# A transformer block on one core: int8 rows set apart, token copies on POOL, maxima over partitions by a PE transposition

## The chip, the cores and the metric

The kernel runs on one core of a Trainium2 chip. A core has TensorE (PE, matmuls; the load of a stationary operand is listed as PEld), VectorE (DVE), ScalarE (ACT), GpSimd (POOL) and SyncE (SP, which here issues DMAs). Each works through its own queue in order, and semaphores hold an instruction back until what it needs is done. [...] The metric is the device time of one execution in microseconds; a comparison takes the median of several runs.

## The reference

The input `x` is 64 sequences of 64 tokens with 256 features, float32. One block is computed:

```python
x = x + attention(rotate(x, delta, amplitudes, frequencies), W_qkv, W_o, log_gamma)
x = x + ffn(masked_pooling(x, W1, b1, v, itok), clip_x, clip_down, w_gate, w_up, w_down)

def act_fake_quant(x, clip):                 # ONE scale for the whole tensor
    scale = sigmoid(clip) * max(abs(x)) / 127
    return clip_(round(x / scale), -128, 127) * scale

def ffn(x, ...):
    xq   = act_fake_quant(x, clip_x)
    gate = xq @ weight_fake_quant(w_gate).T  # 256 -> 704
    up   = xq @ weight_fake_quant(w_up).T
    h    = act_fake_quant(silu(gate) * up, clip_down)
    return h @ weight_fake_quant(w_down).T   # 704 -> 256
```

What matters here is that each activation quantization needs the largest absolute value of a whole tensor, 4096 tokens by 256 and 4096 by 704, before one element of it can be quantized. The two maxima cut the feed-forward part into stages.

## The kernel before

The 4096 tokens are eight groups of 512 (`NG = 8`, `GW = 512`); a group is four tiles of 128 tokens. The first part of the kernel, up to about 239 us of the profile, is attention and the masked pooling, a software pipeline over the groups. It writes the pooled tokens, transposed (features on partitions), to `pooled[g]`, 128 partitions by 2 by 512, float32, and for every group's halves a column of partial maxima to `xam`. The change touches the part after that.

*First scale.* `act_scale(xam, 0, ...)` (lines 96 to 105) reduces `xam` along its row to `mx`, one value per partition, on DVE; POOL's `partition_all_reduce` (line 101) gives every partition the largest of the 128; two small DVE operations make the scale `sx` and its reciprocal `rx`. Ahead of that, ACT loads the table for Silu by a dummy activation (`warm`, line 944).

*Gate stage.* `quantize_tokens(g)` lets ACT multiply a group by `rx` and round it to int8 (`x8`, line 954), and DVE widen that to bf16 (`xq`, line 955). Then come four passes (`j`) over pairs of groups, each over six chunks (`c`) of 128 of the 704 inner features; the last chunk has 64, and the pair's two groups share its 128 partitions. For a chunk PE makes `pg` (gate) and `pu` (up) in PSUM, two buffers each, eight matmuls of 512 columns together (line 978). ACT writes `gate = silu(pg)` (line 986). The product `h` goes to `hT[j]`, by one of two paths: for the chunks in a list, ACT copies `pu` to `up` (line 993) and POOL multiplies (line 996); for the others DVE multiplies straight out of PSUM (line 998). The list has ten of the 24. DVE then takes the largest absolute value of each product into a column of `ham` (`largest`, line 958), two chunks late. After chunks 1 and 3 a group of the next pass is quantized.

*Second scale.* `act_scale(ham, 1, ...)`, the same way, gives `sh` and `rh`.

*Down stage.* `quantize(g)` rounds a group's 704 inner features to int8 on ACT (`h8`, named `h` in the profile, line 1033) and widens it to bf16 on DVE (`hq`, line 1034): five full chunks in one instruction, 5 rows of 512, and for an even group one instruction more, ahead of it, for the shared last chunk of the pair. The first and the last group are done in two halves of 256 tokens. The int8 buffer of a group is 6 rows of 512 bytes without a gap, while in `hq` and `hT` the rows of the pair's two groups alternate, so that a group's rows lie 1024 elements apart there. `down(g)` then multiplies with `wdT`, 24 matmuls of 256 columns (line 1047), scales the result on DVE in two instructions (line 1054) and sends it off. Seven groups go out by a DMA from POOL that adds to what stands in the output (line 1063); the residual was written there earlier. The last group is added on DVE (line 1059) and written by SP in two halves (line 1060).

The order is written out: `manual_schedule` fixes the named engines' queues to the program's order, ACT and DVE in the feed-forward part. PE and POOL there are ordered by a scheduler. In the down stage the program runs `quantize(g)` ahead of `down(g - 1)`.

Of the kernel before, what the change touches and what calls it, by code (L numbers as in the profile page):

```python
# [9 lines left out]
F32 = mybir.dt.float32  # L10
BF16 = mybir.dt.bfloat16
I32 = mybir.dt.int32
I8 = mybir.dt.int8
# [4 lines left out]
P = 128  # L18
# [8 lines left out]
def adaln_attn_ffn(  # L27
# [65 lines left out]
    wscale = const.tile([P, 2, NC], F32, name="wscale")  # L93
    dsc = const.tile([P, D], F32, name="dsc")

    def act_scale(cols, k, scale, inv):

        mx = const.tile([P, 1], F32, name=f"mx{k}")
        nc.vector.tensor_reduce(mx, cols, AX.X, ALU.max)
        allmx = const.tile([P, 1], F32, name=f"allmx{k}")  # L100
        nc.gpsimd.partition_all_reduce(allmx, mx, P, bass_isa.ReduceOp.max)  # L101
        nc.vector.tensor_scalar(
            scale, allmx, csig[:, k : k + 1], 1.0 / QMAX, ALU.mult, ALU.mult
        )
        nc.vector.reciprocal(inv, scale)  # L105


    with ExitStack() as actx:
# [25 lines left out]
        def bank(name):  # L134
            return ps.tile([P, 512], F32, tag="bank", name=name)
# [776 lines left out]
        pooling(a, (1,))  # L912
        pooling_out(a, (1,))


    with ExitStack() as fctx:
        fp = fctx.enter_context(tc.tile_pool(name="ffn", bufs=1))


        assert 2 * LAST == P  # L920
        NP = NG // 2
        NF = 2 * (NC - 1)
        ps_f = ctx.enter_context(ExitStack())
        fw = ps_f.enter_context(tc.tile_pool(name="ffnw", bufs=2))
        ps_g = ps_f.enter_context(
            tc.tile_pool(name="ps_g", bufs=2, space=bass.MemoryType.PSUM)
        )
        xq = fp.tile([P, 2, NT], BF16, name="xq")
        hT = [
            (fp if j < NP - 1 else big).tile(  # L930
                [P, NF + 1, GW], F32, tag=f"hT{j}" if j < NP - 1 else "last", name=f"hT{j}"
            )
            for j in range(NP)
        ]
        ham = fp.tile([P, NP * NC], F32, name="ham")
        ordered = ctx.enter_context(ExitStack())
        ordered.enter_context(
            tc.manual_schedule(
                engines={mybir.EngineType.Activation, mybir.EngineType.DVE}
            )  # L940
        )

        warm = fp.tile([P, 1], F32, name="warm")
        nc.scalar.activation(warm, xam[:, 2 * NG + 1 : 2 * NG + 2], AF.Silu)
        sx = fp.tile([P, 1], F32, name="sx")
        rx = fp.tile([P, 1], F32, name="rx")
        act_scale(xam, 0, sx, rx)
        wsx = fp.tile([P, 2, NC], F32, name="wsx")
        nc.vector.tensor_scalar_mul(wsx, wscale, sx)

        def quantize_tokens(g):

            x8 = fw.tile([P, 2, GW], I8, tag="x8", name=f"x8_{g}")
            nc.scalar.activation(x8, pooled[g], AF.Copy, scale=rx)  # L954
            nc.vector.tensor_copy(xq[:, :, g * GW : (g + 1) * GW], x8)  # L955

        def largest(j, c, h):
            nc.vector.tensor_reduce(  # L958
                ham[:, j * NC + c : j * NC + c + 1], h, AX.XY, ALU.max,
                apply_absolute_value=True,  # L960
            )

        quantize_tokens(0)
        quantize_tokens(1)


        late = []
        for j in range(NP):
            for c in range(NC):
                wide = c < NC - 1  # L970
                n = 2 if wide else 1
                pg = ps_g.tile([P, 2, GW], F32, tag="pg", name=f"pg_{j}_{c}")
                pu = ps_g.tile([P, 2, GW], F32, tag="pu", name=f"pu_{j}_{c}")
                for dst, w in ((pg, wgT), (pu, wuT)):
                    for kc in range(2):
                        for k in range(2):
                            g = 2 * j + k
                            nc.tensor.matmul(  # L978
                                dst[:, k, :] if wide else dst[k * LAST : (k + 1) * LAST, 0, :],
                                w[:, kc, c * P : min((c + 1) * P, FF)],  # L980
                                xq[:, kc, g * GW : (g + 1) * GW],
                                start=(kc == 0),
                                stop=(kc == 1),
                            )
                gate = fw.tile([P, 2, GW], F32, tag="gate", name=f"gate_{j}_{c}", bufs=3)
                nc.scalar.activation(  # L986
                    gate[:, :n], pg[:, :n], AF.Silu, scale=wsx[:, 0, c : c + 1]
                )
                h = hT[j][:, 2 * c : 2 * c + n, :]

                if wide and c in ((0, 2, 4), (1, 3), (0, 2, 4), (0, 2))[j]:
                    up = fw.tile([P, 2, GW], F32, tag="up", name=f"up_{j}_{c}")
                    nc.scalar.activation(  # L993
                        up, pu, AF.Copy, scale=wsx[:, 1, c : c + 1]
                    )
                    nc.gpsimd.tensor_tensor(h, gate, up, ALU.mult)  # L996
                else:
                    nc.vector.scalar_tensor_tensor(  # L998
                        h, pu[:, :n], wsx[:, 1, c : c + 1], gate[:, :n], ALU.mult, ALU.mult
                    )  # L1000
                late.append((j, c, h))
                if len(late) > 2:
                    largest(*late.pop(0))
                if c in (1, 3) and j + 1 < NP:
                    quantize_tokens(2 * (j + 1) + c // 2)
        for l in late:
            largest(*l)
        ps_f.close()
        fw = fctx.enter_context(tc.tile_pool(name="ffnd", bufs=2))
        ps_d = fctx.enter_context(  # L1010
            tc.tile_pool(name="ps_d", bufs=4, space=bass.MemoryType.PSUM)
        )

        sh = fp.tile([P, 1], F32, name="sh")
        rh = fp.tile([P, 1], F32, name="rh")
        act_scale(ham, 1, sh, rh)

        hq = {}

        def quantize(g):  # L1020

            j, k = divmod(g, 2)
            if k == 0:
                hq[j] = fw.tile([P, NF + 1, GW], BF16, tag="hq", name=f"hq_{j}")
            h8 = fw.tile([P, NC, GW], I8, tag="h8", name=f"h8_{g}")
            parts = 2 if g in (0, NG - 1) else 1
            for r in range(parts):
                cols = slice(r * (GW // parts), (r + 1) * (GW // parts))
                for rows, tmp in (
                    (slice(NF, NF + 1), h8[:, NC - 1 : NC, cols]),  # L1030
                    (slice(k, NF, 2), h8[:, 0 : NC - 1, cols]),
                )[k:]:
                    nc.scalar.activation(tmp, hT[j][:, rows, cols], AF.Copy, scale=rh)  # L1033
                    nc.vector.tensor_copy(hq[j][:, rows, cols], tmp)  # L1034

        def down(g):
            j, k = divmod(g, 2)

            res = xg[0 if g == NG - 1 else g]
            for r in range(2):  # L1040
                tiles = slice(2 * r, 2 * r + 2)
                pdn = ps_d.tile([P, 2, D], F32, tag="pdn", name=f"pdn_{g}_{r}")
                for i in range(2):
                    tok = slice((2 * r + i) * P, (2 * r + i + 1) * P)
                    for c in range(NC):
                        half = slice(0, P) if c < NC - 1 else slice(k * LAST, (k + 1) * LAST)
                        nc.tensor.matmul(  # L1047
                            pdn[:, i, :],
                            hq[j][half, 2 * c + k if c < NC - 1 else NF, tok],
                            wdT[half, c, :],  # L1050
                            start=(c == 0),
                            stop=(c == NC - 1),
                        )
                nc.vector.tensor_tensor(  # L1054
                    res[:, tiles], pdn, dsc.unsqueeze(1).to_broadcast([P, 2, D]), ALU.mult
                )
                if g == NG - 1:
                    xr = xg[g][:, tiles, :]
                    nc.vector.tensor_tensor(xr, xr, res[:, tiles], ALU.add)  # L1059
                    nc.sync.dma_start(out=ot[g][:, tiles, :], in_=xr)  # L1060
            if g < NG - 1:

                nc.gpsimd.dma_start(out=ot[g], in_=res, accum_op=ALU.add)

        for g in range(NG + 1):
            if g < NG:
                quantize(g)
            if g == 0:
                nc.vector.tensor_scalar_mul(dsc, dsc, sh)
            else:  # L1070
                down(g - 1)
        ordered.close()
# [44 lines left out]
```

## Time and profile before

| what | value |
|---|---|
| median of three runs | 339.9 us (339.25 to 340.07) |
| the profiled execution, own time | 340.35 us |
| its span, first to last instruction | 338.6 us |
| granted PE clock, mean | 0.959 |
| busy: PE, DVE, ACT, POOL | 285.5, 253.8, 197.6, 77.8 us |
| first scale, `mx` starts | 239.3 us |
| gate stage, first `x8` to last maximum | 240.7 to 295.0 us |
| second scale, `rh` ends | 296.1 us |
| down stage, first `h` to the last DVE instruction | 296.2 to 333.9 us |

All times come from one profiled execution. A group row of the profile names line, engine, operation, output and inputs, shapes and count; behind the bar stand the busy time, the mean of one in ns, and the idle time of the engine ahead of it with what ended it. A timeline row gives start and duration in us and merges like instructions; in brackets stands the idle time ahead of it. Lines of the changed kernel have other numbers; the names stay.

### The profile page before, as it was taken

What the parts mean: (1) busy time and instruction counts of PE and PEld (TensorE: products, weight loads), DVE (VectorE), ACT (ScalarE), POOL (GpSimd) and SP (SyncE); (2) the same over time, 40 slices, a digit from 0 to 9 for tenths busy, and PEclk for the clock granted to TensorE, in tenths of its full rate; (3) what the DMA queues carried; (4) which work ended last, traced back from release to release, by engine and by line L of the source; (5) the groups of instructions that cost most, each with busy time, mean ns of one, the idle gap of its engine ahead of it and who ended that gap; (6) DMA issues with size and microseconds to landing.
All of it is one profiled execution on the core that took longest, in us unless ns stands there. A gap on an engine that the chain in (4) does not pass through costs nothing. (4 is left out here: it accounts for less than half of the span.)

```text
span 338.6 us, 8695 instructions
## 1 busy us (share of the span) xinstructions
PE 285.5 (84%) x3762; PEld 194.5 (57%) x3762; DVE 253.8 (75%) x510; ACT 197.6 (58%) x299; POOL 77.8 (23%) x72
## 2 busy tenths in 40 slices
PE   0499999999999999989999999784499889168892
PEld 0386768668668758848858858563243334034451
DVE  6569886886976974884883783856359999969993
ACT  1566458568477483673673573332598798196620
POOL 0051330240240230112012021040055358003331
PEclk9999999999999999999999999997599999859997
DMA  5491721001001001000100100100000000005999
GB/s 157 118 339 34 202 73 62 5 2 64 3 2 63 4 0 42 26 2 3 66 0 2 66 2 11 56 0 3 2 0 0 1 2 0 0 0 67 131 123 177
DMA packets 16789, 16.15 MB, mean 48 GB/s; under 512 B 2160, under 2 KB 16496, under 8 KB 16752
## 3 DMA queue, kind: packets, MB, share of 16 engines
q1 hardware_dynamic: 12480, 11.83, 11.3%
q0 software_dynamic: 3696, 3.67, 8.1%
q8 instruction: 29, 0.48, 0.6%
q10 hardware_dynamic: 576, 0.11, 0.2%
q14 instruction: 8, 0.07, 0.1%
HBM read 7.74 MB, written 7.86 MB: 46 GB/s over the span
## 5 line engine op out<-in xcount | busy, mean ns | idle before, releaser
L334 DVE TENSOR_TENSOR at<-psc,gam 128x512 f32<-128x512 f32 x64 | 39.7, 681 | 14.6 <-PE psc L321 14.6
L1047 PE MATMUL pdn<-wdT,hq 128*128 128x256 bf16 x192 | 30.4, 291 | 13.2 <-DVE hq L1034 13.2
L386 PE MATMUL po<-woT,yT 128*128 128x256 f32 x128 | 31.1, 386 | 5.2 <-DVE kn L252 2.7
L152 POOL TENSOR_TENSOR ys<-x,cs 128x1024 f32<-128x1024 f32 x7 | 13.8, 1967 | 89.8 <-DVE xr L166 67.4
L1047 PEld LDWEIGHTS <-hq 128*128 128x128 bf16 x192 | 16.7, 101 | 27.2 <-DVE hq L1034 14.8
L206 PE MATMUL pk<-wkT,xT 128*128 128x256 f32 x128 | 30.0, 388 | 0.2 <-ACT xT L196 0.2
L978 PE MATMUL pg<-xq,wgT 128*128 128x512 bf16 (+1 forms) x96 | 25.1, 391 | 5.9 <-DVE xq L955 5.1
L206 PE MATMUL pv<-wvT,xT 128*128 128x256 f32 x128 | 29.8, 386 | 0.1
L996 POOL TENSOR_TENSOR hT<-gate,up 128x1024 f32<-128x1024 f32 x10 | 24.1, 2410 | 24.0 <-ACT up L993 24.0
L386 PEld LDWEIGHTS po<-woT,yT 128*128 128x128 f32 x128 | 23.1, 190 | 11.2 <-DVE kn L252 5.1
L281 PE MATMUL pq<-xT,wqT 128*128 128x512 f32 x64 | 29.5, 604 | 0.0
L1033 ACT ACTIVATE h<-hT,rh 128x2560 int8<-128x2560 f32 (+3 forms) x15 | 22.2, 1538 | 12.5 <-DVE rh L105 7.0
L986 ACT ACTIVATE gate<-pg,wsx 128x1024 f32<-128x1024 f32 (+1 forms) x24 | 25.0, 1053 | 6.0 <-PE pg L978 3.6
L978 PE MATMUL pu<-xq,wuT 128*128 128x512 bf16 (+1 forms) x96 | 24.6, 390 | 2.3 <-ACT up L993 1.3
L206 PEld LDWEIGHTS pk<-wkT,xT 128*128 128x128 f32 x128 | 24.2, 195 | 3.9 <-ACT xT L196 0.9
L958 DVE TENSOR_REDUCE ham<-hT 128x1 f32<-128x1024 f32 (+1 forms) x24 | 26.3, 1118 | 0.0
L206 PEld LDWEIGHTS pv<-wvT,xT 128*128 128x128 f32 x128 | 23.7, 190 | 4.5 <-issue 1.4
L408 POOL TENSOR_TENSOR bias<-pre,sel 128x256 f32<-128x256 f32 x8 | 4.9, 612 | 86.7 <-DVE ms L457 86.7
L1034 DVE CAST hq<-h 128x2560 bf16<-128x2560 int8 (+3 forms) x15 | 22.2, 1509 | 3.2 <-ACT h L1033 3.2
L289 ACT ACTIVATE qbd<-pq,hm 128x512 f32<-128x512 f32 x32 | 20.1, 680 | 4.9 <-PE pq L281 4.8
L321 PE MATMUL psc<-qbd,kT 32*64 32x128 f32 x1024 | 20.7, 279 | 0.6 <-DVE at L334 0.3
L998 DVE SCALAR_TENSOR_TENSOR hT<-pu,wsx,gate 128x1024 f32<-128x1024 f32 (+1 forms) x14 | 15.7, 1124 | 6.3 <-ACT gate L986 6.3
(177 smaller groups left out, 530.4 us busy)
## 6 DMA issues: line engine op xcount, KB each, us to landing
x<-in_x_dram SPq DMA_DIRECT2D x8, 512.0 KB, 6.4
out_dram<-x SPq DMA_DIRECT2D x7, 512.0 KB, 3.9
out_dram<-x POOLq DMA_DIRECT2D x7, 512.0 KB, 6.1
wq_nat<-in_L_attn_W_qkv_dram SPq DMA_DIRECT2D x3, 256.0 KB, 8.8
wnat_d<-in_L_ffn_w_down_dram SPq DMA_DIRECT2D x1, 704.0 KB, 7.0
wnat<-in_L_ffn_w_gate_dram SPq DMA_DIRECT2D x1, 640.0 KB, 4.9
wnat<-in_L_ffn_w_up_dram SPq DMA_DIRECT2D x1, 640.0 KB, 6.6
out_dram<-x SPq DMA_DIRECT2D x2, 256.0 KB, 4.3
```

Of the source, the lines that this page charges most:

```text
L206: nc.tensor.matmul(pk[:, i * D : (i + 1) * D], xT[:, kc, t * P : (t + 1) * P], w[:, kc, :], start=(kc == 0), stop=(kc == 1),)
L281: nc.tensor.matmul(pq, wqT[:, kc, hf * P : (hf + 1) * P], xT[:, kc, :], start=(kc == 0), stop=(kc == 1),)
L321: nc.tensor.matmul(banks[p][k * S : (k + 1) * S, i, hf, :], kT[rows, hf, b * S : (b + 1) * S], qbd[rows, hf, b].rearrange("p k t -> p (k t)"),
L334: nc.vector.tensor_tensor(at[:, p].rearrange("p i f k t -> p i (f k t)"), banks[p].rearrange("p i f c -> p i (f c)"), gam[:, p] .rearrange ...
L386: nc.tensor.matmul(po[:, i * D : (i + 1) * D], yT[:, i, hf].rearrange("p k t -> p (k t)"), woT[:, hf, :], start=(hf == 0), stop=(hf == 1),)
L958: nc.vector.tensor_reduce(ham[:, j * NC + c : j * NC + c + 1], h, AX.XY, ALU.max, apply_absolute_value=True,)
L978: nc.tensor.matmul(dst[:, k, :] if wide else dst[k * LAST : (k + 1) * LAST, 0, :], w[:, kc, c * P : min((c + 1) * P, FF)], xq[:, kc, g * G ...
L986: nc.scalar.activation(gate[:, :n], pg[:, :n], AF.Silu, scale=wsx[:, 0, c : c + 1])
L996: nc.gpsimd.tensor_tensor(h, gate, up, ALU.mult)
L1033: nc.scalar.activation(tmp, hT[j][:, rows, cols], AF.Copy, scale=rh)
L1034: nc.vector.tensor_copy(hq[j][:, rows, cols], tmp)
L1047: nc.tensor.matmul(pdn[:, i, :], hq[j][half, 2 * c + k if c < NC - 1 else NF, tok], wdT[half, c, :], start=(c == 0), stop=(c == NC - 1),)
```

## The change

Five edits go together.

- `act_scale` gets a PSUM tile. PE transposes `mx`, read as 128 equal columns, against the identity, so that every partition holds all 128 values in a row, and DVE reduces that row. `partition_all_reduce` goes. The first call, with `warm`, moves to the end of the attention part's written-out order; `pmx_0` takes one of that part's PSUM banks, `pmx_1` a buffer of the down stage's pool.
- The first two groups' tokens are quantized in four pieces, feature half by feature half, with four `x8` buffers; they are widened on DVE. `wsx` comes after them in DVE's queue.
- The other six groups' widening copies are POOL's, whose queue is now written out too: a copy comes after the multiplies that stand ahead of it in the program.
- The list of chunks multiplied on POOL is chunks 0, 2, 4 in even passes and 1, 3 in odd ones: again ten, in the last pass 1 and 3 in place of 0 and 2.
- `h8` has rows of 576, of which 512 are used. The first group is rounded and widened in pieces of 128, 128 and 256 tokens.

```diff
-    def act_scale(cols, k, scale, inv):
+    def act_scale(cols, k, scale, inv, pt):
         mx = const.tile([P, 1], F32, name=f"mx{k}")
         nc.vector.tensor_reduce(mx, cols, AX.X, ALU.max)
         allmx = const.tile([P, 1], F32, name=f"allmx{k}")
-        nc.gpsimd.partition_all_reduce(allmx, mx, P, bass_isa.ReduceOp.max)
+        nc.tensor.transpose(pt, mx.to_broadcast([P, P]), ident)
+        nc.vector.tensor_reduce(allmx, pt, AX.X, ALU.max)
...
+        warm = const.tile([P, 1], F32, name="warm")
+        nc.scalar.activation(warm, xam[:, 2 * NG + 1 : 2 * NG + 2], AF.Silu)
...
+        act_scale(xam, 0, sx, rx, bank("pmx_0")[:, 0:P])
...
-                engines={mybir.EngineType.Activation, mybir.EngineType.DVE}
+                engines={
+                    mybir.EngineType.Activation,
+                    mybir.EngineType.DVE,
+                    mybir.EngineType.Pool,
+                }
...
-        nc.vector.tensor_scalar_mul(wsx, wscale, sx)
-        def quantize_tokens(g):
-            x8 = fw.tile([P, 2, GW], I8, tag="x8", name=f"x8_{g}")
-            nc.scalar.activation(x8, pooled[g], AF.Copy, scale=rx)
-            nc.vector.tensor_copy(xq[:, :, g * GW : (g + 1) * GW], x8)
+        def quantize_tokens(g, kcs=slice(0, 2)):
+            x8 = fw.tile([P, 2, GW], I8, tag="x8", name=f"x8_{g}_{kcs.start}", bufs=4)
+            nc.scalar.activation(x8[:, kcs], pooled[g][:, kcs], AF.Copy, scale=rx)
+            widen = nc.vector if g < 2 else nc.gpsimd
+            widen.tensor_copy(xq[:, kcs, g * GW : (g + 1) * GW], x8[:, kcs])
+        for kc in range(2):
+            for g in range(2):
+                quantize_tokens(g, slice(kc, kc + 1))
+        nc.vector.tensor_scalar_mul(wsx, wscale, sx)
...
-                if wide and c in ((0, 2, 4), (1, 3), (0, 2, 4), (0, 2))[j]:
+                if wide and c in ((0, 2, 4), (1, 3))[j % 2]:
...
-        act_scale(ham, 1, sh, rh)
+        pmx = ps_d.tile([P, P], F32, tag="pmx", name="pmx_1", bufs=1)
+        act_scale(ham[:, 0:nham], 1, sh, rh, pmx)
...
-            h8 = fw.tile([P, NC, GW], I8, tag="h8", name=f"h8_{g}")
-            parts = 2 if g in (0, NG - 1) else 1
-            for r in range(parts):
-                cols = slice(r * (GW // parts), (r + 1) * (GW // parts))
+            h8 = fw.tile([P, NC, GW + 64], I8, tag="h8", name=f"h8_{g}")
+            at = 0
+            for n in (1, 1, 2) if g == 0 else (2, 2) if g == NG - 1 else (4,):
+                cols = slice(at * P, (at + n) * P)
+                at += n
```

`largest` now counts its own columns, which changes no instruction.

More of the change, by code (lines that the diff above doesn't have):

```diff
@@ L913, in adaln_attn_ffn @@
         pooling_out(a, (1,))
+        warm = const.tile([P, 1], F32, name="warm")
+        nc.scalar.activation(warm, xam[:, 2 * NG + 1 : 2 * NG + 2], AF.Silu)
+        sx = const.tile([P, 1], F32, name="sx")
+        rx = const.tile([P, 1], F32, name="rx")
+        act_scale(xam, 0, sx, rx, bank("pmx_0")[:, 0:P])
     with ExitStack() as fctx:
@@ L938, in adaln_attn_ffn, with largest @@
             tc.manual_schedule(
-                engines={mybir.EngineType.Activation, mybir.EngineType.DVE}
-            )
-        )
[L943 to L947, printed above, removed]
-        wsx = fp.tile([P, 2, NC], F32, name="wsx")
-        nc.vector.tensor_scalar_mul(wsx, wscale, sx)
-        def quantize_tokens(g):
-            x8 = fw.tile([P, 2, GW], I8, tag="x8", name=f"x8_{g}")
-            nc.scalar.activation(x8, pooled[g], AF.Copy, scale=rx)
-            nc.vector.tensor_copy(xq[:, :, g * GW : (g + 1) * GW], x8)
-        def largest(j, c, h):
+                engines={
[3 more added lines that the diff above has]
+                }
+            )
+        )
+        wsx = fp.tile([P, 2, NC], F32, name="wsx")
+        def quantize_tokens(g, kcs=slice(0, 2)):
[6 more added lines that the diff above has]
+                quantize_tokens(g, slice(kc, kc + 1))
+        nc.vector.tensor_scalar_mul(wsx, wscale, sx)
+        nham = 0
+        def largest(h):
+            nonlocal nham
             nc.vector.tensor_reduce(
-                ham[:, j * NC + c : j * NC + c + 1], h, AX.XY, ALU.max,
-                apply_absolute_value=True,
-            )
-        quantize_tokens(0)
-        quantize_tokens(1)
+                ham[:, nham : nham + 1], h, AX.XY, ALU.max, apply_absolute_value=True
+            )
+            nham += 1
         late = []
@@ L1000, in adaln_attn_ffn @@
                     )
-                late.append((j, c, h))
+                late.append(h)
                 if len(late) > 2:
-                    largest(*late.pop(0))
+                    largest(late.pop(0))
                 if c in (1, 3) and j + 1 < NP:
                     quantize_tokens(2 * (j + 1) + c // 2)
-        for l in late:
-            largest(*l)
+        for h in late:
+            largest(h)
         ps_f.close()
```

## The prediction

> **What bounds the kernel now.** I read the page first, for its chain, then the groups kept apart by shape, then the timeline of the last 100 us, and last the table of windows, for the DMA.
>
> ```profile
> span 338.6 us, 8695 instructions
> DVE hq L1034 4%; ACT gate L986 3%; PE pdn L1047 2%; DVE x L1054 2%; PE pg L978 2%; ACT x L954 2%; PE pu L978 2%; ACT h L1033 2%; ACT up L993 2%; DVE hT L998 1%; POOL hT L996 1%; DVE xq L955 0%; DVE ham L958 0%; DVE x L1059 0%; POOL allmx L101 0%
> ```
>
> The costliest line of the chain is the widening copy `hq<-h`. Its shapes, from the groups of the last 100 us (name, shapes, count, then busy us and mean ns):
>
> ```profile
> L1034 DVE CAST hq<-h 128x2560 bf16<-128x2560 int8 x6 | 16.9, 2812 | 1.1 <-ACT h L1033 1.1
> L955 DVE CAST xq<-x 128x1024 bf16<-128x1024 int8 x8 | 7.0, 870 | 1.7 <-ACT x L954 1.7
> L1034 DVE CAST hq<-h 128x1280 bf16<-128x1280 int8 x4 | 3.9, 985 | 1.5 <-ACT h L1033 1.5
> L684 POOL TENSOR_SCALAR_AFFINE_SELECT gam<-gam 64x1024 f32<-64x1024 f32 x2 | 2.3, 1148 | 1.8 <-ACT gam L681 1.7
> ```
>
> Twice the elements (1280 to 2560) cost 2.9 times the time: 1.10 ns each against 0.77. The down stage, one pair of groups, from the timeline (start, duration, engine):
>
> ```profile
> 304.71 1.28 DVE L1054 TENSOR_TENSOR x<-pdn,dsc 128x512 f32<-128x512 f32 x2
> 305.91 3.14 DVE L1034 CAST hq<-h 128x512 bf16<-128x512 int8 x2
> 308.97 1.28 DVE L1054 TENSOR_TENSOR x<-pdn,dsc 128x512 f32<-128x512 f32 x2
> 309.11 3.53 PE L1047 MATMUL pdn<-wdT,hq 128*128 128x256 bf16 x24 [0.73 <-DVE hq L1034]
> 310.16 2.81 DVE L1034 CAST hq<-h 128x2560 bf16<-128x2560 int8 x1
> 312.89 1.28 DVE L1054 TENSOR_TENSOR x<-pdn,dsc 128x512 f32<-128x512 f32 x2
> 313.03 3.52 PE L1047 MATMUL pdn<-wdT,hq 128*128 128x256 bf16 x24 [0.40 <-DVE hq L1034]
> ```
>
> DVE runs without a hole: 304.71 to 312.89 is 8.18 us for two groups, 4.09 each. PE needs 3.49 a group (`325.46 6.98`, x48, in the same view) and waits for `hq` at each. So DVE bounds this stage.
>
> The gate stage, 240.74 to 294.97, has the same owner: from 248.60 on, DVE's idle entries add up to 1.3 us in 46. PE's last matmul ends at 288.8; then DVE works off multiplies and maxima until 294.97. One line shows what the tokens' copies cost there:
>
> ```profile
> 260.55 2.42 POOL L996 TENSOR_TENSOR hT<-gate,up 128x1024 f32<-128x1024 f32 x1 [2.39 <-ACT up L993]
> 261.54 1.98 DVE L955 CAST xq<-x 128x1024 bf16<-128x1024 int8 x1
> 264.76 1.02 PE L978 MATMUL pu<-xq,wuT 128*128 128x512 bf16 x4 [0.82 <-DVE hT L998]
> ```
>
> A copy of 0.68 us took 1.98: it ended 0.5 us after POOL's multiply did. PE then stood 0.82 us.
>
> [...]the whole int8 block is one run of 2560 while its destination has 5 rows[...]; the half-width pieces are 5 rows of 256 on both sides[...] The multiply here takes 2.41 us for 1024; POOL's one-input select takes 1.15.
>
> **The change, part by part.** Times after `rh` or `rx` are taken from those instructions' ends (296.11 and 240.43).
>
> *Rows set apart.* `h8` rows become 576 wide, so source and destination are both 5 rows of 512[...]. In the steady pairs DVE then needs 8.18 - 2 x 1.06 = 6.06 us, PE 6.98, ACT (2.42 + 0.72 + 2.42, each overlapping the next by 0.1) 5.3. PE becomes the bound, with about 0.7 us to spare before each copy is missed. ACT's rows are strided now; I charge nothing, its half-width forms (1.35 us for 1280) lie on the same line as 2560 (2.42).
>
> *First group in pieces 1, 1, 2.* ACT's rows give 0.29 + 0.83 ns an element. Small piece 0.40, then 5 x 128 in 0.82[...]: PE starts 0.10 + 0.30 + 0.82 + 0.05 + 0.55 + 0.05 = 1.87 us after `rh`, before 2.91. At PE's half clock a 128-token tile takes 1.43 (5.73 / 4). The third tile waits for the 1280 copy (4.9), so the group ends at 7.8. Group 1 needs ACT's sixth and seventh pieces (end 6.2, with two instructions more, 0.3 us later than now) and 1.75 of copy: PE starts it at 8.05, before 8.74. **-0.7.** Seven groups follow: before 304.85 to 332.46 = 27.6, after 7 x 3.49 = 24.4. **-3.2.**
>
> *What the writes give back.* Each group's accumulating DMA is already close behind the last one:
>
> ```profile
> core 0: us, PE busy (x) PEld busy (x) DVE busy (x) ACT busy (x) POOL busy (x), PEclk, DMA share, GB/s
> 320.00:324.00 4.00, 3.60 (x26) 2.08 (x25) 4.00 (x5) 2.92 (x3) 1.27 (x1) 1.00 0.98 130
> 334.00:335.00 1.00, 0.00 (x0) 0.00 (x0) 0.00 (x0) 0.00 (x0) 0.00 (x0) 1.00 1.24 200
> ```
>
> Seven DMAs take 8.1% of the span, 3.9 us of all engines each; with a group every 3.49 us they queue. If 3.9 is firm, 7 x 3.9 plus the last two writes ends only 0.7 us earlier than now, and 3.2 us are lost. But the last row carries 200 GB/s where the steady ones carry 130, so some of 3.9 is latency that a queue hides. Bounds 0 to 3.2; I take **+0.6**. POOL's issue (1.28 us) took 1.52 and 1.59[...]; 0.3 us on a DMA that queues anyway: nothing.
>
> *Maxima by PE.* Now `mx` end to `sx` start is 0.56 us (239.46 to 240.02), and 0.55 the second time. In its place: a transposition and a PSUM reduction of 128 columns. The transposition of `pp` near 236 took 0.63 from DVE's end to DVE's next start, a 128-column reduction 0.28: 0.94. First time, +0.38 less the 0.31 us that ACT's table load already runs past `rx` (ACT starts at 240.74): **+0.1**. Second time PE is at half clock after 5 us of rest: +0.4 to 0.6, **+0.45**. Bounds 0 and 1.0 in all. On PE nothing but the next stage's matmuls is queued behind either transposition; they need its result anyway. On POOL the all-reduce stood ahead of the hidden multiplies and of the output DMAs, hundreds of nanoseconds that nobody waited for.
>
> *Tokens in four half copies.* Two ACT pieces of 0.72 in place of 1.15, DVE 0.42 in place of 0.69: PE starts 1.25 us after ACT does, before 1.9; the fourth piece arrives at 3.1 as before at 2.9. The first gate starts some 0.7 earlier. `wsx` waits behind four copies and still comes before the first gate.
>
> *Six copies to POOL.* DVE loses 0.87 + 0.68 + 1.98 + 3 x 0.68 = 5.6 us (5.1 without overlaps). POOL gains six copies; no row shows one[...]. I take 1.15, the select's row. POOL's order is multiply, copy, multiply: `x8_5` stands behind the multiply of pass 1's fourth chunk, so PE waits there about 1.2 us. I laid all rows of this stage in queue order with 0.05 us per hand-over. For before this ends 54.4 us after ACT's start (measured 54.23), for after 52.4: PE's holes at `pu<-hT` shrink, ACT becomes near-critical (pass 0 holds 10.8 us of ACT work, PE's 48 matmuls 10.35), and the tail from the last gate (two multiplies' remainder and three maxima, 4 us) stays. **-1.9**, start included. At 1.6 us a copy this is -0.7; at 2.0, +1.4; at 2.4, +3.8. Ten multiplies stay on POOL, the last pass has chunks 1 and 3 in place of 0 and 2.
>
> Sum: -0.7 - 3.2 + 0.6 + 0.1 + 0.45 - 1.9 = **-4.65**. The profiled execution took 340.35 (1.75 around its span): 335.7. It lay 0.45 above the median of the three runs, 339.9, from which the forecast is **335.3**. Less than 0.3%, 1.0 us, can't be told from no change here.
>
> **Rivals.** *POOL's copy is dear* (the one that ends slower): above 2.2 us each, PE waits for `xq` at all three pass borders and ACT behind it, and -1.9 turns into over +2.7. At 2.4: -4.65 + 5.7, 341.0. For it: POOL's two-input rows, and int8 may be dearer than f32; against: the select. *The copy stays[...]* (the rows apart don't count): no 3.2, group 1 starts 0.4 later instead of 0.7 earlier; with the rest -1.0, 338.9. Against it stand the 985 ns rows, whose source already lies apart. *The writes bind*: 2.6 more given back, 337.9. For it the DMA share of 0.98, against it the 200 GB/s.
>
> **How the numbers follow.** Forecast 0.66 (own range 334.2 to 336.8: the writes and PE's clock, which leaves half speed at a varying moment, ±0.7 us); writes bind 0.15; dear copy 0.12 (a third of it still faster, at 1.5 to 1.8 us)[...]. Range 333.3 to 338.7. Faster: 0.66 + 0.15 + 0.03 + 0.01 = 0.85; same 0.06[...]; slower 0.09.
>
> **What would show it.** Casts of 2560 at 1.75 us, and PE without a hole from group 1 to 7 (else the first step is wrong). The first `pdn` matmul 1.9 us after `rh`. POOL's copies near 1.15; if over 2, holes before `pg` at each pass. `sh` 0.9 to 1.1 us after `mx`. The gate stage from ACT's start to the last `ham` near 52.4. DMA share at 1 up to the end with the last landing later than 5.5 us after PE's end would mean the writes bind.

## The result, and the profile after

The changed kernel takes **337.05 us** (median of four, 336.96 to 337.29). The kernel before takes 339.66 beside it (339.25 to 340.07). The ratio is 0.9924, 95% interval 0.9907 to 0.9942: faster by 2.6 us. The forecast was 335.3, 4.6 us under the median then known (339.9). The measured time lies inside the range of 333.3 to 338.7 but above the forecast's own 334.2 to 336.8. The profiled execution took 336.96, its span is 3.4 us shorter. The page's first line and its chain by lines:

```profile
span 335.2 us, 8697 instructions
...
PE po L388 9%; PE pv L208 9%; PE pdn L1060 7%; PE pk L208 6%; PE psc L323 4%; PE py L361 4%; DVE at L336 4%; ACT gate L997 3%; ACT L238 3%; PE pl L511 3%; DMA afb<-n_L_cond_amplitudes_dram 3%; PE pa L433 2%; POOL hT L1006 2%; ACT up L1003 2%; DVE xam L528 2%
```

The widening copy `hq`, 4% of the span in the chain before, no longer stands among these lines: one cast of 1.77 us is left of it, ahead of PE's start on group 1. PE's `pdn` has 7%, 2% before. (The list before followed the chain back only to 240.8 us, this one to the start of the kernel, so the other lines can't be set against each other.) The groups of the last 100 us, by shape (count, then busy us and mean ns):

```profile
L1047 DVE CAST hq<-h 128x2560 bf16<-128x2560 int8 x6 | 10.5, 1750 | 1.1 <-ACT h L1046 1.1
...
L961 POOL CAST xq<-x 128x1024 bf16<-128x1024 int8 x6 | 6.2, 1036 | 0.0
```

2812 ns has become 1750, as the forecast had it. By the access patterns that the trace keeps for these casts, the int8 source was one run of 2560 and is now 5 rows of 512, like the destination in both kernels; that this alone makes the difference, experiments 2 and 3 show. POOL's copy takes 1036. The down stage in the timeline, the last piece of group 0 and the first groups after it:

```profile
304.78 8.39 PE L1060 MATMUL pdn<-wdT,hq 128*128 128x256 bf16 x58 [0.25 <-DVE hq L1047]
...
305.83 2.08 DVE L1047 CAST hq<-h 128x512 bf16<-128x512 int8 x2
...
309.02 1.75 DVE L1047 CAST hq<-h 128x2560 bf16<-128x2560 int8 x1
...
311.80 0.69 DVE L1067 TENSOR_TENSOR x<-pdn,dsc 128x512 f32<-128x512 f32 x1 [0.44 <-PE pdn L1060]
```

From 304.78 PE runs on without a wait, and it is DVE that waits for PE (the last line). The two have changed places. The table of windows, with the DMA's share behind the clock:

```profile
core 0: us, PE busy (x) PEld busy (x) DVE busy (x) ACT busy (x) POOL busy (x), PEclk, DMA share, GB/s
...
324.00:328.00 4.00, 4.00 (x30) 2.30 (x28) 2.65 (x4) 0.00 (x0) 1.95 (x2) 1.00 1.21 181
```

The gate stage shows what went wrong. Its first six microseconds:

```profile
240.42 2.56 ACT L959 ACTIVATE x<-pooled_a,rx 128x512 int8<-128x512 f32 x4 [0.62 <-DVE rx L107]
...
242.55 1.06 PE L989 MATMUL pg<-xq,wgT 128*128 128x512 bf16 x2 [0.22 <-issue]
...
243.40 0.63 PE L989 MATMUL pu<-xq,wuT 128*128 128x512 bf16 x1
...
243.83 1.06 PE L989 MATMUL pg<-xq,wgT 128*128 128x512 bf16 x2
...
246.25 1.11 ACT L997 ACTIVATE gate<-pg,wsx 128x1024 f32<-128x1024 f32 x1 [3.28 <-PE pg L989]
```

PE is never idle here for long, and yet ACT's first gate starts 5.83 us after the first `x8`. PE's queue deals out `pg_0`, `pu_0` and `pg_1` in turn. (By the order of the weight loads, an entry of `x2` holds one matmul of `pg_1` and one of `pg_0`; the record of the first `pu` is missing.) So the fourth matmul of `pg_0`, which releases the gate, is PE's tenth. PE is at half clock here (the granted clock is 0.5 until 246.05), and a matmul takes 0.43 us. In the kernel before the gate waited for PE's fifth matmul.

Where the time went, from the two profiled executions:

| stretch | before | after | difference | forecast |
|---|---|---|---|---|
| up to `mx` of the first scale (same code) | 239.29 | 238.82 | -0.47 | 0 |
| first scale, `mx` to ACT's first `x8` | 1.45 | 1.60 | +0.15 | +0.1 |
| gate stage, to the last `ham` | 54.20 | 54.71 | **+0.5** | **-1.9** |
| second scale, `mx` end to `sh` | 0.55 | 0.96 | +0.41 | +0.45 |
| `rh` end to PE's start of group 1 | 8.74 | 8.07 | -0.67 | -0.7 |
| seven groups on PE | 27.61 | 24.27 | -3.34 | -3.2 |
| PE's end to the end of the span | 6.14 | 6.15 | 0.0 | +0.6 |

The rows add up to -3.4. The medians differ by 2.6, since the profiled execution of before was 0.7 above its median. The first row is scatter: over all the profiles of this document `mx` starts between 238.55 and 239.79 us. So a difference of about a microsecond between two single executions says little, and the comparisons below go by stage.

### The profile page after: what moved, and what is told of

Read it like the earlier page. It is cut to its first block, busy times and chain, and to the rows that moved or that the text cites. A ratio compares the mean times of both kernels' runs of the same rounds, so it can differ in the third digit from the quotient of the medians.

```text
span 335.2 us, 8697 instructions
## 1 busy us (share of the span) xinstructions
PE 286.9 (86%) x3760; PEld 194.9 (58%) x3764; DVE 244.2 (73%) x510; ACT 197.6 (59%) x303; POOL 84.9 (25%) x76
## 4 chain that ended last, share of the span: by engine, by line
PE 53%; DVE 21%; ACT 15%; issue 5%; DMA 3%; POOL 2%; ACTq 0%; DVEq 0%
PE po L388 9%; PE pv L208 9%; PE pdn L1060 7%; PE pk L208 6%; PE psc L323 4%; PE py L361 4%; DVE at L336 4%; ACT gate L997 3%; ACT L238 3%; PE pl L511 3%; DMA afb<-n_L_cond_amplitudes_dram 3%; PE pa L433 2%; POOL hT L1006 2%; ACT up L1003 2%; DVE xam L528 2%
## 5 line engine op out<-in xcount | busy, mean ns | idle before, releaser
L1006 POOL TENSOR_TENSOR hT<-gate,up 128x1024 f32<-128x1024 f32 x10 | 23.7, 2370 | 37.3 <-ACT up L1003 37.3
L989 PE MATMUL pg<-xq,wgT 128*128 128x512 bf16 (+1 forms) x94 | 25.9, 399 | 4.7 <-DVE xq L961 2.2
L1046 ACT ACTIVATE h<-hT,rh 128x2560 int8<-128x2560 f32 (+5 forms) x17 | 22.3, 1387 | 8.5 <-DVE rh L107 7.3
L989 PE MATMUL pu<-xq,wuT 128*128 128x512 bf16 (+1 forms) x94 | 23.6, 385 | 1.7 <-DVE hT L1008 1.7
L377 ACT ACTIVATE yT<-py,hm 128x256 f32<-128x256 f32 x32 | 13.4, 470 | 11.5 <-PE py L361 11.5
```

The source lines that it names most:

```text
L989: nc.tensor.matmul(dst[:, k, :] if wide else dst[k * LAST : (k + 1) * LAST, 0, :], w[:, kc, c * P : min((c + 1) * P, FF)], xq[:, kc, g * G ...
```

## The experiments

All changes are to the changed kernel unless said; "kernel 1" is the kernel of experiment 1, and so on. Kernels 1 to 4 ran beside the kernel before at 339.80 us, 5 to 8 at 339.97 and 9 to 11 at 340.36; the ratios are to that.

**1. PE's queue written out.** Theory: the order above costs the gate stage's start. Rival: PE must wait for the half copies whatever its order.

```diff
                 engines={
+                    mybir.EngineType.PE,
                     mybir.EngineType.Activation,
```

> The changed kernel with PE's queue of the feed-forward part written out in program order too (four matmuls of pg, four of pu, chunk after chunk). Theory (PE's order): in the changed kernel the scheduler dealt pg_0, pu_0 and pg_1 in turn, so that the first gate waited for the tenth matmul at half clock; in program order the fourth matmul ends 3.5 us after ACT's first x8, the first gate starts at 3.6 in place of 5.8, the gate stage shrinks from 54.7 to 52.4 us, and the time is 334.9 us (2.2 below 337.05). Rival (the half clock and the data hold the first gate, whatever the order): the first gate stays above 5 us, the time within 0.5 us of 337.05. Rival (PE's work is the same, so what starts earlier waits later): first gate at 3.6 but last maximum no earlier, 337.

Measured: 334.64 us (334.31 to 335.08), ratio 0.9852 (0.9835 to 0.9869). Its timeline:

```profile
241.70 2.33 PE L990 MATMUL pg<-xq,wgT 128*128 128x512 bf16 x4 [2.22 <-DVE xq L962]
...
243.82 1.91 PE L990 MATMUL pu<-xq,wuT 128*128 128x512 bf16 x4
...
244.11 1.11 ACT L998 ACTIVATE gate<-pg,wsx 128x1024 f32<-128x1024 f32 x1 [1.18 <-PE pg L990]
```

The same four matmuls in a row, and the gate starts 3.73 us after ACT's first `x8` (240.38) instead of 5.83. The gate stage takes 52.90 us, 1.8 less. The theory holds: one line in the list of engines is worth 2.4 us in the medians, nearly as much as the whole change, and 1.8 of it is seen in this stage.

**2. Only the rows set apart**, in the kernel before.

```diff
-            h8 = fw.tile([P, NC, GW], I8, tag="h8", name=f"h8_{g}")
+            h8 = fw.tile([P, NC, GW + 64], I8, tag="h8", name=f"h8_{g}")
```

> The kernel before with one edit: rows of h8 576 wide. Theory[...]: whole casts 1750 ns in place of 2812, PE without a hole from group 1 on, 7 groups in 24.4 us in place of 27.6; group 1 still starts at PE's own end of group 0 (8.7 after rh); 339.7 - 3.2 = 336.5 us. Rival (most of the gain came from the tokens' copies and the first group's pieces): 338.5 us or more. Rival (the writes bind): 337.5 with the last landing later than 6 us after PE's end.

Measured: 336.16 us (334.82 to 336.93), 0.9893 (0.9875 to 0.9911). This one edit takes off 3.6 us; the four others together add nothing to it (337.05 against 336.16, with intervals of the ratios that just overlap). Between the two profiles the others lengthen the gate stage by 0.5 us and the two scales by 0.15 and 0.41, and shorten the way from `rh` to PE's end by 0.65 (32.99 to 32.34 us).

**3. All but the rows set apart.** The edit of 2 the other way round.

> The changed kernel with h8 rows of 512 without a gap again. Theory: casts of 2812 ns, DVE bounds the down stage again, group 1 starts 9.1 us after rh in place of 8.0, seven groups take 27.6 in place of 24.3: 337.05 + 4.4 = 341.4 us, slower than the kernel before. Rival (the writes would have held the changed kernel nearly as far back): 339 or less.

Measured: 341.28 us (340.53 to 341.53), 1.0043 (1.0028 to 1.0058): slower than the kernel before. In its timeline the copy is dear again and PE waits for it at group 1:

```profile
302.65 2.82 DVE L1047 CAST hq<-h 128x2560 bf16<-128x2560 int8 x1 [1.10 <-ACT h L1046]
...
305.52 3.52 PE L1060 MATMUL pdn<-wdT,hq 128*128 128x256 bf16 x24 [1.38 <-DVE hq L1047]
```

**4. The all-reduce in place of the transposition.**

```diff
-        nc.tensor.transpose(pt, mx.to_broadcast([P, P]), ident)
-        nc.vector.tensor_reduce(allmx, pt, AX.X, ALU.max)
+        nc.gpsimd.partition_all_reduce(allmx, mx, P, bass_isa.ReduceOp.max)
...
```

> The changed kernel with the maxima over partitions by POOL's partition_all_reduce again, all else as changed. Theory: from mx's end to the scale 0.55 us in place of 0.96 at the second scale and 0.56 in place of 0.9 at the first, where ACT's table load hides half: 0.15 + 0.41 less, 336.5 us. Rival (the difference is hidden[...]): 337.05 within 0.2.

Measured: 335.86 us (335.57 to 336.43), 0.9884 (0.9867 to 0.9902). It does not tell the two ways apart: without the transposition the scheduler dealt PE's matmuls out in another order (three of `pg_0` first), and the gate started 3.99 us after ACT. But it showed something that the forecast had not reckoned with. The second scale took 1.22 us from the end of `mx` to `sh`, not 0.55. From the all-reduce's line of code and the timeline:

```profile
L102 POOLq MODIFY_POOL_CONFIG  x4: 13/18/22, 223.3 to 288.3; - x4
```
```profile
285.70 2.41 POOL L1005 TENSOR_TENSOR hT<-gate,up 128x1024 f32<-128x1024 f32 x1 [0.67 <-ACT up L1002]
...
293.95 0.38 POOL L102 PARTITION_ALL_REDUCE allmx<-mx  x1 [5.84 <-DVE mx L99]
```

The last `MODIFY_POOL_CONFIG` of the all-reduce's line is issued at 288.33, right after the end of the last multiply (288.11), and the all-reduce starts 5.62 us after the issue although `mx` was there at 293.14, 0.81 us earlier. So the releaser in the brackets is not what ended the wait. In the kernel before the last `MODIFY_POOL_CONFIG` stands at 288.3 too, but `mx` came at 295.15, 7.0 us after the last multiply, and the all-reduce followed it by 0.14 us.

**5. PE's order and the all-reduce**, 1 and 4 together, to have both on one order of PE.

> e1_pe_order with POOL's partition_all_reduce in place of the transposition. e4_allreduce had the scale 1.22 us after mx, not 0.55[...]. Theory[...]: at the second scale sh comes 5.6 + 0.4 us after POOL's last multiply, about 1.1 us after mx, no better than the transposition's 0.96; at the first scale 0.3 us better, of which ACT's table load leaves 0.2: 334.4 us, within 0.3 of e1_pe_order. Rival (the all-reduce is really 0.55 and e4's 1.22 a chance): 334.0 or below.

Measured: 335.82 us (334.94 to 336.44), 0.9875 (0.9851 to 0.9899). Gate stage 52.88, as in 1. The all-reduce started 5.7 us after the last `MODIFY_POOL_CONFIG` (289.4 to 295.07), 5.87 after the last multiply's end, and `sh` 1.36 us after `mx`, 0.4 later than with the transposition; at the first scale, where POOL had rested for 15 us, `mx` to ACT was 1.25, 0.35 sooner. The expected gain isn't there: each way wins one scale, and the all-reduce lost where `mx` came 4.9 us after POOL's last multiply. That the total lies 1.2 above 1 is not explained by these two; in the profiled execution 1.0 of it lies in the attention part, whose code is the same.

**6. PE's order, and all token copies back on DVE.**

```diff
-            widen = nc.vector if g < 2 else nc.gpsimd
+            widen = nc.vector
```

> e1_pe_order with the six tokens' copies on DVE again, in place of POOL. Theory: DVE gets 6 x 0.68 us back plus waits of up to 1.3 us behind POOL's multiplies; POOL's queue no longer holds x8_5 behind a multiply, so that PE's wait at the third pass (about 1 us) goes. Laid out in queue order the gate stage ends 0.9 us later: 335.5 us. Rival (the copies on POOL are worth the 5.1 us that they take off DVE): 338 or more. Rival (they are worth nothing, or less): 334.6 or below.

Measured: 336.68 us (335.31 to 337.13), 0.9892 (0.9868 to 0.9917). The gate stage takes 53.23 us, only 0.33 more than in 1 and 0.47 more than in the repeat of 1 below; 0.9 was expected. The rest of the total's 2.0 us is elsewhere, as far as a profile shows it: in this one PE stayed at half clock for 9.7 us of the down stage (3.8 in 1; the granted clock from 302 to 306 is 0.50 against 1.00), and its end came 33.90 us after `rh` against 32.34. So in this order the six copies on POOL are worth 0.3 to 0.5 us of the gate stage, not the 1.2 that the forecast left for the stage beyond its start. The other five executions have no profile; what holds their median up is not shown.

**7. PE's order, and the first two groups' tokens in whole copies.**

```diff
-        for kc in range(2):
-            for g in range(2):
-                quantize_tokens(g, slice(kc, kc + 1))
+        for g in range(2):
+            quantize_tokens(g)
```

> e1_pe_order with the first two groups' tokens quantized whole, as before the change. Theory: PE starts 1.9 us after ACT in place of 1.3, the first gate at 4.4 in place of 3.7, the gate stage 0.7 us longer: 335.3 us. Rival (the stage is paced by ACT and DVE later, the start doesn't count): 334.6 within 0.3.

Measured: 336.19 us (335.82 to 338.52), 0.9897 (0.9866 to 0.9928). The first gate starts 4.49 us after ACT, 0.76 later than with half copies, and the stage takes 53.50, 0.60 longer. The half copies are worth what the forecast said, if PE's order lets them be. The total lies 1.55 us over that of kernel 1; in the profiled executions 0.7 of the rest is in the attention part, whose code is the same.

**8. PE's order, and the second pass's token copies one chunk earlier**, ahead of POOL's multiply instead of behind it.

```diff
-                if c in (1, 3) and j + 1 < NP:
+                if c in ((1, 3), (0, 2))[j % 2] and j + 1 < NP:
```

> e1_pe_order with the tokens quantized after chunks 0 and 2 in place of 1 and 3 in the odd passes, so that POOL's copy stands ahead of a multiply and not behind it. Theory: PE's wait of 1 us for x8_5's copy at the start of the third pass goes, and what it delays; laid out in queue order the gate stage is 1.4 us shorter: 333.2 us. Rival (ACT is the bound there, the wait only moves): 334.6 within 0.4.

Measured: **332.74 us** (331.54 to 334.44), 0.9788 (0.9759 to 0.9817). The wait that this takes away, in the timeline of the changed kernel:

```profile
267.48 1.03 POOL L961 CAST xq<-x 128x1024 bf16<-128x1024 int8 x1
...
268.57 1.46 PE L989 MATMUL pg<-xq,wgT 128*128 128x512 bf16 x5 [0.98 <-POOL xq L961]
```

ACT had that copy's int8 ready at 266.14, but POOL's multiply ran until 267.53. In the groups of the gate stage by shape, kernel 1 and then kernel 8:

```profile
L990 PE MATMUL pg<-xq,wgT 128*128 128x512 bf16 x80 | 22.5, 393 | 4.4 <-DVE xq L962 2.2 <-POOL xq L962 1.0 <-ACT gate L998 0.9
```
```profile
L990 PE MATMUL pg<-xq,wgT 128*128 128x512 bf16 x78 | 22.0, 392 | 2.9 <-DVE xq L962 2.2 <-ACT gate L998 0.4
```

No wait for POOL is left, and the stage is 1.9 us shorter (50.97), twice the wait. The theory accounts for only half of that, for the edit moves ACT's rounding (`x`) a chunk earlier too. The second pass in the repeats of kernels 1 and 8 below, kernel 1 first:

```profile
257.52 1.11 ACT L998 ACTIVATE gate<-pg,wsx 128x1024 f32<-128x1024 f32 x1 [0.89 <-POOL hT L1007]
...
259.53 1.15 ACT L960 ACTIVATE x<-pooled_a,rx 128x1024 int8<-128x1024 f32 x1
```
```profile
256.27 1.19 ACT L960 ACTIVATE x<-pooled_a,rx 128x1024 int8<-128x1024 f32 x1
257.32 1.15 ACT L998 ACTIVATE gate<-pg,wsx 128x1024 f32<-128x1024 f32 x1
```

In kernel 1 ACT waits 0.89 us for POOL and later rounds a group ahead of the third chunk's gate; in kernel 8 the rounding fills that hole. In the second pass the third chunk's gate comes 0.97 us sooner (19.09 us after the first `x8` against 20.06), before PE has reached the POOL copy; the third pass's first gate comes 1.80 sooner (25.75 against 27.55), and this stays to the end. No kernel moves one of the two alone, and none has the earlier rounding with all copies on DVE.

**9 to 11, on one chip:** the rows and PE's order alone, in the kernel before, and kernels 1 and 8 again. The first one's edits are the row of experiment 2 and

```diff
-                engines={mybir.EngineType.Activation, mybir.EngineType.DVE}
+                engines={mybir.EngineType.PE, mybir.EngineType.Activation, mybir.EngineType.DVE}
```

> The kernel before with two of the ideas only: the int8 rows set apart, and PE's queue in the feed-forward part written out. Theory (PE's dealt-out order costs time at half clock): in the kernel before the first gate waits for the fifth matmul instead of the fourth, two of them of the second weight, so writing the order out takes 0.4 to 0.8 us off the start of the gate stage: 335.4, where the rows alone gave 336.2. The rest of the change (half copies, POOL copies, pieces, transposition) is then worth under 1 us against 334.6 of the changed kernel with PE's order. Rival (PE's order matters only to the changed kernel's half copies): 336.2, no difference from the rows alone.

> The changed kernel with PE's queue written out, once more, on the same chip as the next one, so that the two can be compared: 334.6 as before; gate stage 52.9 us.

> The same, with the token copies of the second pass a chunk earlier, ahead of POOL's multiplies. Theory (the POOL copy behind a multiply holds PE at the third pass): PE has no wait for a POOL copy, gate stage 51.0, total 1.9 below the run before it: 332.7. Rival (the 1.9 was a scatter of the first look): 334.6.

| kernel | us | ratio to before | gate stage |
|---|---|---|---|
| rows and PE's order, in the kernel before | 337.60 (336.53 to 337.97) | 0.9911 (0.9894 to 0.9929) | 55.35 |
| kernel 1 again | 334.78 (334.15 to 335.20) | 0.9835 (0.9818 to 0.9852) | 52.76 |
| kernel 8 again | 332.83 (332.11 to 334.52) | 0.9786 (0.9763 to 0.9808) | 50.96 |

The last two come out as expected, and the intervals of their ratios lie apart: kernel 8 is the best version, over 7 us under the kernel before. The first is a miss. PE's order alone brings the kernel before nothing at the start of the gate stage; here the rival was right, and its timeline says why:

```profile
242.37 0.69 DVE L955 CAST xq<-x 128x1024 bf16<-128x1024 int8 x1 [0.34 <-ACT x L954]
243.11 1.44 PE L978 MATMUL pg<-xq,wgT 128*128 128x512 bf16 x3 [0.43 <-DVE xq L955]
```

With whole copies PE has to wait for group 1's tokens in the middle of `pg_0`. The matmul of `pu_0` that the scheduler had put there filled this hole, so the first gate starts 4.48 us after ACT either way. With half copies the interleaving cost 2.10 us (5.83 against 3.73).

The stage is 1.15 us longer than in the kernel before, and this can't be put down to the order. Every gate from the second on is 0.9 to 1.2 us later (the second 7.84 us after the first `x8` against 6.72, the last 48.90 against 47.74), so the loss arises in the first chunks, where PE was at half clock for longer in this execution: the granted clock is still 0.50 up to 248, 7.8 us after the first `x8` (240.16), and in the kernel before it is 1.00 from 246.4 on, 5.7 us after (in the changed kernel from 246.05, 5.6 after). Two windows of equal length, this kernel and then the kernel before (columns as in the table of windows above; PEclk is the third figure from the end):

```profile
246.00:248.00 2.00, 2.00 (x6) 0.76 (x5) 0.00 (x0) 1.11 (x1) 0.45 (x1) 0.50 0.00 0
```
```profile
246.40:248.40 2.00, 2.00 (x11) 0.88 (x9) 0.00 (x0) 1.95 (x2) 0.69 (x1) 1.00 0.00 0
```

PE's waits for `xq` over the stage grow too, from 5.1 to 6.9 us, but the gates fall no further behind by them.

## Why the prediction was right or wrong

**Tokens in four half copies, and the gate stage's -1.9: the step that failed.** "PE starts 1.25 us after ACT does" came true (241.74 is 1.32 after 240.42). "The first gate starts some 0.7 earlier" did not: it started 1.35 later, 5.83 against 4.48. The forecast took PE's order as it had been, though PE was not among the engines with a written order and its scheduler sees new operands. Kernel 1 restores the step: 3.73, 0.75 earlier. That is 2.1 of the 2.4 us by which the stage missed. From the first gate to the last maximum the changed kernel needs 48.88 us, the kernel before 49.72: 0.8 less, where the forecast had 1.2.

**Six copies to POOL: the mechanism was right, the size was not.** 1036 ns a copy against 1.15 us assumed, 1.01 ns an element, where POOL's two-input multiply takes 2370 for as many. The wait behind the multiply is there, 0.98 us against 1.2. But DVE's freed 5 us bought little. The sums of the windows from 248.6 to 288 us (39.4 us), before and then after, in the columns PE, PEld, DVE, ACT, POOL:

```profile
sum 39.40, PE 35.87 PEld 14.96 DVE 38.05 ACT 35.72 POOL 23.09; mean PE 11.96 PEld 4.99 DVE 12.69 ACT 11.91 POOL 7.70
```
```profile
sum 39.40, PE 35.35 PEld 14.43 DVE 33.23 ACT 35.52 POOL 27.16; mean PE 11.78 PEld 4.81 DVE 11.08 ACT 11.84 POOL 9.05
```

DVE's busy time falls by 4.8 us and becomes idle time; PE and ACT do no more work than before. They were only 3.5 and 3.7 us from full, so a stage that DVE bounded went at once to one in which PE, ACT and POOL wait for each other. Kernel 6 puts the copies' worth at 0.3 to 0.5 us as the queues stood, and kernel 8 shows what their order still held back: 1.9. What the new list of chunks in the last pass and the later `wsx` did was not tried alone.

**Rows set apart: right**, and kernels 2 and 3 show it alone: 3.6 us with it, and without it slower than before. That is the forecast's own -3.2 and more. The 1750 ns were the author's estimate, and no trace of the kernel before shows what they rested on; that they came out to the nanosecond is luck. From that kernel's rows alone an estimate comes to between 1700 and 1970: the undisturbed tokens' copies take 680 to 688 ns for 1024 elements, 0.67 each, and the half-width pieces, whose source lies in 5 rows already, 985 for 1280, 0.77 each.

**First group in pieces: right.** PE starts 1.97 us after `rh` (1.87 foreseen; the 0.55 in that sum for the first copy of 5 x 128 was an estimate too, and the two of that size took 557 ns on average), group 1 at 8.07 (8.05). **Maxima by PE: right**, +0.15 and +0.41. What was not seen is that the all-reduce takes longer where POOL's last multiply ends closer to `mx`: 1.22 and 1.36 us from `mx` to `sh` where 5.0 and 4.9 us lie between (kernels 4 and 5), 0.55 where 7.0 do (the kernel before). With that, the two scales of kernels 1 and 5 put the two ways level (0.35 lost, 0.41 won), where the prediction's sum had the transposition 0.55 behind.

**What the writes give back: over-sized.** +0.6 was taken, 0.0 came. PE's end to the span's end is 6.15 us as before, and between 5.7 and 6.2 in kernels 1 to 8. The 181 GB/s in the window of 324 to 328 decide between the two readings of the 3.9 us a DMA: 512 KB in 3.9 us would be 134, so 3.9 was not firm with a group every 3.47 us. The sign that the prediction set for *The writes bind* was a last landing over 5.5 us after PE's end; the last packet ends 4.96 us after it in both kernels. POOL's issues got slower, 1.36 to 1.69 us on average, as foreseen (beside the casts of 1750 ns 1.61 to 1.95, with no cast beside it 1.28), and nobody waited for them. In the kernel before the two slow issues had different neighbours: beside the one of 1.52 ran two casts of 1280 elements (1.94 us together), beside the one of 1.59 a cast of 2560 in 2.8 us, and beside four more casts of that length the issues took 1.27 to 1.28.

So the sum -4.65 became -2.95 (and -0.47 of scatter in unchanged code): -1.9 turned into +0.5, a loss of 2.4, and 0.6 that wasn't taken came back. That the total still fell inside the range is in part luck: one term had the wrong sign, and another that was too cautious made up for a quarter of it. It ended near the number of *The writes bind* (337.9) for another reason. The rivals "dear copy", "the copy stays" (0.07 of the forecast) and "the writes bind" are all out, by 1036 ns, 1750 ns and the unchanged 4.96 us.

## What to carry to other kernels

When an edit makes operands arrive in another grain or earlier, look at how the queue of the engine that uses them is ordered afterwards; an order left to a scheduler is part of what the edit changes, and the first output needs its own matmuls first. Freeing the busiest engine need not buy its time, here 0.3 to 0.5 us of 5; look in the same trace for who waits then, and move the work that stands ahead of that wait, which brought 1.9 more. And look at how the two sides of a copy fall into rows: one merged run of 2560 against 5 rows took 1.10 ns an element, 1.06 us a copy more than 5 rows against 5 (0.68 ns), while one run of 1024 against 2 rows took 0.67 ns (680 to 688 for 1024). Last, before a stage of one execution is called longer, look at how long PE was at half clock in it.

## What was not expected of the hardware

From the last `MODIFY_POOL_CONFIG` to the all-reduce's start it took 5.62 us (kernel 4) and 5.7 us (kernel 5), though `mx` was there 0.81 and 0.94 us before that start. The instruction itself lasted 11 to 25 ns, and no row of the profile is busy on POOL in between. In the kernel before 7.0 us lay between the two, and the all-reduce started 0.14 us after `mx`. What fills the 5.6 us is not shown.

PE's stay at half clock at the start of the down stage lasted 3.3 us (kernel 7), 3.4 (kernel 1 again), 3.8 (kernel 1), 5.4 (the changed kernel, and kernel 8 again) and 9.7 (kernel 6), with the same instructions on PE in that stage. In the changed kernel the granted clock is 0.50 from 293.83 to 304.07, 10.24 us, and in the kernel before, also for 10.24 us, from 294.08 to 304.32. The half clock begins there while PE rests (in the kernel before its last matmul of the gate stage ends at 288.81), and the stay is what was left of it when PE's first `pdn` started (298.68 in the changed kernel). Why it lasted longer in kernel 6 is open. There PE's end came 33.90 us after `rh`, and with stays of 3.3, 3.8 and 5.4 us in the same down stage 32.34. So a single execution can move by 1.5 us with PE's clock, and stages were compared here, not totals, where less than that mattered.
